# The second attention layer's first 512 destinations: from dense products to row gathers

## The chip, the cores and the metric

The kernel runs on one core of a Trainium2 chip. TensorE multiplies matrices into PSUM, VectorE and ScalarE do elementwise work, GpSimd (POOL in the profile) does small elementwise work and issues indirect DMAs, and SyncE (SP) issues most plain DMAs. The engines run side by side[...] and wait for one another through semaphores. The metric is the device time of one execution in microseconds (us), as a median over runs. Before the change it is 1865.05 us (three runs, 1863.82 to 1865.54).

## The reference

A graph has N = 3125 nodes with 256 features and 103125 edges (50000 random pairs in both directions, and a loop at each node), sorted by destination. A node thus has 33 incoming edges on average. Four blocks follow one another: three attention layers (GAT), a mixture of 16 experts, a plain graph sum, and a top-1 mixture of 8. Only the second attention layer changes. One such layer is

```python
h = x @ W;  el = h @ al;  er = h @ ar
e = leaky_relu(el[src] + er[dst], 0.2)
alpha = softmax of e over the edges of each dst
out = segment_sum(alpha[:, None] * h[src], dst) + b
```

With exp taken out of the leaky relu, an edge's weight is a product of a factor of the source and max(tau of the destination, rho of the source), where rho = exp(0.8 el) and tau = exp(-0.8 er); a factor of the destination alone cancels in the softmax. So the layer needs, for each destination, the sum over its edges of max(tau, rho) times the source's row, and the same sum of weights to divide by.

## The kernel before

**Dense layers.** The nodes are cut into 25 tiles of 128 (the last has 53). While layer 1 runs, the kernel counts how many edges lead from each source to each destination and keeps the counts as bytes in SBUF (`counts`). Each layer then treats the graph as dense. It walks over 13 groups of 256 destinations (`GROUPS`; the last has 53), and within a group over the 25 source tiles (`for s in range(NT)` in `dense_attention`). For each source tile VectorE makes `pm` = max(tau, rho) * counts, 128 sources by 256 destinations (line 1310), and TensorE multiplies it in two halves with the source tile's rows `h`, 256 features and one column of weights, into `acc` (line 1313). The buffers for `pm` are six. tau of the next group comes from two transposes at step 18 (`terms`, lines 1250 and 1253).

**Going onward.** When a group is through, `divide` (lines 1339 to 1348) normalises its sums on VectorE during the next group's step 8, and at steps 10 and 13 `onward` transposes each tile, applies relu on ScalarE and calls `put` (lines 1142 to 1149) of the next layer's `Sources`. `put` multiplies by the next weights, clamps the two scores on VectorE (line 1145), and writes rho, the weight column and the scaled row `h` on ScalarE. `h` is a tile of 25 x 257 floats per partition; rho is a tile of its own. The last tile of a layer goes onward at step 10 of the next layer's first group.

**Lists and counts.** `Locator` gathers pieces of the sorted edge list for windows of five destinations, 125 windows at a time: `find` computes where each begins (`at`) and issues two indirect DMAs of 125 rows of 275 integers (line 1590), `finish` decodes them. `Counter` makes one-hot matrices on VectorE (line 1668) and ScalarE, and multiplies them on TensorE into `counts` (line 1683). This takes place ahead of and during layer 1.

**Queues around it.** During layer 1 SP also writes filler rows into the expert buffers (`spare_rows`, line 1727; three writes in each group, released by two small GpSimd writes, line 1320). The router of layer 3 gets its constants by DMA (lines 579 to 585). In layer 3 GpSimd scatters each node's row of 258 floats to two experts (line 676). The order within each engine's queue is not quite that of the source text: the building layer reorders instructions by its own estimate of when each is ready, and what it decides is fixed before the run.

Of the kernel before, what the change touches and what calls it, by code (L numbers as in the profile page):

```python
# [9 lines left out]
F32 = mybir.dt.float32  # L10
F16 = mybir.dt.float16
BF16 = mybir.dt.bfloat16
I32 = mybir.dt.int32
# [3 lines left out]
OP = mybir.AluOpType  # L17
# [705 lines left out]
def routed_experts(tc, x, room, ident, rows, sums, places, w1, w2, w3, load):  # L723
# [10 lines left out]
    with tc.tile_pool(name="rw", bufs=3) as ep, tc.tile_pool(name="rx", bufs=2) as xp, \  # L734
# [99 lines left out]
        def turn_more(slot, xs, s, own):  # L834
            ps = tp.tile([P, nh, P], F32, name="ps_x")
            for j in range(nh):
                nc.tensor.transpose(ps[:, j], s[:, j * P:(j + 1) * P], ident)
            hid = mp.tile([P, nh, P], F32, name="hid1")
            nc.scalar.copy(hid, ps)
            return slot, xs, hid, own  # L840

# [235 lines left out]
TERMS = 18  # L1077
EARLY = 8
SOME = 6
HELD = 64.0  # L1080


# [32 lines left out]

def block(big, d=D):

    return big.tile([P, NT * (D + 1)], F32, name="big")[:, :NT * d].rearrange("p (t d) -> p t d", d=d)


class Sources:
# [2 lines left out]

    def __init__(self, tc, big, small):
        self.nc = tc.nc
        self.h = block(big, D + 1)
        self.rho = small.tile([P, NT], F32, name="rho")
        self.lr = small.tile([P, 2, NT], F32, name="lr")

        for to in (self.h[:, NT - 1], self.rho[:, NT - 1:], self.lr[:, :, NT - 1]):
            self.nc.gpsimd.memset(to, 0.0)

    def put(self, pp, t, r, xTs, w, at=()):


        nc, n = self.nc, len(xTs)
        pss = []
        for i, xT in enumerate(xTs):
            ps = at[i] if i < len(at) else pp.tile([P, D + 2], F32, name="ps_m")  # L1140
            for k in range(KD):
                nc.tensor.matmul(ps[:r], xT[:, k], w[:, k], start=(k == 0), stop=(k == KD - 1))
            pss.append(ps)
        for i, ps in enumerate(pss):
            nc.vector.tensor_scalar(self.lr[:r, :, t + i], ps[:r, D:], -HELD, HELD, op0=OP.max, op1=OP.min)
        nc.scalar.activation(self.h[:r, t:t + n, D], self.lr[:r, 0, t:t + n], AF.Exp, scale=0.2)
        nc.scalar.activation(self.rho[:r, t:t + n], self.lr[:r, 0, t:t + n], AF.Exp, scale=0.8)
        for i, ps in enumerate(pss):
            nc.scalar.activation(self.h[:r, t + i, :D], ps[:r, :D], AF.Copy, scale=self.h[:r, t + i, D:])


def dense_attention(tc, dram, counts, x_in, big, ident, eps, layers, src, dst, rows, high, make_router, over):

# [6 lines left out]
    nc = tc.nc  # L1162
    with tc.tile_pool(name="dw", bufs=1) as cp, tc.tile_pool(name="dwl", bufs=2) as wl, \
         tc.tile_pool(name="dsm", bufs=2) as small:
        top = cp.tile([P, 3], F32, name="top")
        x = block(big)
        with tc.tile_pool(name="dp", bufs=6) as pmp, tc.tile_pool(name="ds", bufs=2) as sp, \
             tc.tile_pool(name="dpa", bufs=2, space=PSUM) as ap_, \
# [8 lines left out]
            ohp = first.enter_context(tc.tile_pool(name="doh", bufs=2))  # L1177
            kp = first.enter_context(tc.tile_pool(name="dpc", bufs=2, space=PSUM))
            counter = Counter(tc, lp, ohp, locator, counts)
            pairs = [range(-(-c // (BATCH * WIN)), -(-(c + n) // (BATCH * WIN))) for c, n in GROUPS]  # L1180


# [76 lines left out]
            for i in range(3):  # L1259
                last = i == 2  # L1260
                bt_i = bt
                if last:
                    wp = third.enter_context(tc.tile_pool(name="ro", bufs=2))
                    rp = third.enter_context(tc.tile_pool(name="ror", bufs=4))
                    zp = third.enter_context(tc.tile_pool(name="rop", bufs=1, space=PSUM))
                    router = make_router(third.enter_context(tc.tile_pool(name="roc", bufs=1)))
                    y_out = block(big)
                    nc.gpsimd.memset(y_out[:, NT - 1], 0.0)
                    nxt, we_n = None, None
                else:  # L1270
                    nxt = Sources(tc, big, small)
                    we_n, bt, products = attention_weights(tc, wl, cp, layers, i + 1, now.rho[:, NT - 1:])
                    products()
                for a, (c, n) in enumerate(GROUPS):
                    tiles = [(q, (c + q) // P, min(P, n - q)) for q in range(0, n, P)]

                    edges = counts_of(counts, a)
                    ahead = list(pairs[a + 1]) if i == 0 and a + 1 < len(GROUPS) else []
                    ready = []
                    tau = tau_next if a else terms(now, 0)  # L1280
                    acc = ap_.tile([P, 2, CHUNK], F32, name="acc")
                    rest = []
                    if last:
# [5 lines left out]
                    for s in range(NT):  # L1289
# [8 lines left out]
                        if n <= P // 2:  # L1298
                            if s % SOME == 0:
                                m = min(SOME, NT - s)  # L1300
                                few = sp.tile([P, SOME, n], F32, name="few")
                                nc.vector.tensor_tensor(few[:, :m], tau[:, None, :n].to_broadcast([P, m, n]),
                                                        now.rho[:, s:s + m, None].to_broadcast([P, m, n]), op=OP.max)
                                nc.vector.tensor_tensor(few[:, :m], few[:, :m], edges[:, s:s + m, :n], op=OP.mult)
                            at = s % 2 * (P // 2)
                            nc.tensor.matmul(acc[at:at + n, 0, :D + 1], few[:, s % SOME], now.h[:, s], start=(s < 2),
                                             stop=(s >= NT - 2))
                        else:
                            pm = pmp.tile([P, PAIR], F32, name="pm")
                            nc.vector.scalar_tensor_tensor(pm[:, :n], tau[:, :n], now.rho[:, s:s + 1],  # L1310
                                                           edges[:, s, :n], op0=OP.max, op1=OP.mult)
                            for j, (q, t, r) in enumerate(tiles):
                                nc.tensor.matmul(acc[:r, j, :D + 1], pm[:, q:q + r], now.h[:, s], start=(s == 0),  # L1313
                                                 stop=(s == NT - 1))
                        while ready and ready[0][0] <= s:
                            counter.add(kp, ready.pop(0)[1])
                        if s == 2 and fills:

                            for e in empties:
                                nc.gpsimd.tensor_scalar(e, tau[:, 0:1], 0.0, None, op0=OP.mult)  # L1320
# [34 lines left out]
                        norm, gate, send = router.group(wp, rp, zp, y_out, tiles[0][1], len(tiles))  # L1355
                        later += [(9 - sooner, norm), (11 - sooner, gate), (14 - sooner, send)]
                    for j, (q, t, r) in enumerate(tiles if not last else []):
                        def onward(j=j, t=t, r=r, rest=rest, nxt=nxt, w=we_n):
                            ps = pp.tile([P, KD, P], F32, name="ps_m")
                            for k in range(KD):  # L1360
                                nc.tensor.transpose(ps[:, k, :r], rest[j][:r, k * P:(k + 1) * P], ident[:r, :r])  # L1361
                            yT = sp.tile([P, KD, P], F32, name=f"yT{j}")
                            nc.scalar.activation(yT[:, :, :r], ps[:, :, :r], AF.Relu)  # L1363
                            nxt.put(pp, t, r, [yT[:, :, :r]], w)
                        later.append((10 + 3 * j, onward))
                    if i == 0 and a == 1:
                        fills, empties = spare_rows(tc, cp, *rows)
                if i == 0:
                    first.close()
                nc.vector.tensor_reduce(top[:, i:i + 1], now.lr, AX.XY, OP.max, apply_absolute_value=True)  # L1370
                now = nxt
            for _, what in later:
                what()
            router.finish(wp, zp, over)
            ps = pp.tile([3, P], F32, name="ps_m")
            nc.tensor.transpose(ps, top, ident)
            most = cp.tile([3, 1], F32, name="most")
            nc.vector.tensor_reduce(most, ps, AX.X, OP.max)
            ps = pp.tile([1, 3], F32, name="ps_m")
            nc.tensor.transpose(ps, most, ident[:3, :3])  # L1380
            nc.vector.tensor_reduce(high, ps, AX.X, OP.max)
            third.close()
    return y_out
# [135 lines left out]
class Locator:  # L1519
# [8 lines left out]
    def __init__(self, tc, cp, dram, src, dst, ident, room):  # L1528
# [36 lines left out]
        def find(j, pp, behind=None):  # L1565
# [8 lines left out]
            for q in range(NHEAD):  # L1574
                nc.tensor.matmul(ps[:PW], less[:rows, q, :PW], one[:rows], start=(q == 0), stop=(q == NHEAD - 1))
            at = cp.tile([P, 1], I32, name=f"at{j}")
            nc.vector.tensor_scalar(at[:PW], ps[:PW], -1.0, 0.0, op0=OP.add, op1=OP.max)
            if j < PARTS - 1:
                nc.vector.tensor_scalar(at[:PW], at[:PW], float(NR - RE // ER), None, op0=OP.min)
            for u, (of, name) in enumerate(self.lists):  # L1580
                if j == PARTS - 1:

                    to = dram.tile([E + RE], I32, name=name)
                    nc.sync.dma_start(to[:E].rearrange("(p e) -> p e", p=rows), of.rearrange("(p e) -> p e", p=rows))
                    none = cp.tile([1, RE], I32, name=name)
                    nc.gpsimd.memset(none, -WIN)
                    nc.sync.dma_start(to[None, E:], none)
                    of = to
                of = of.rearrange("(t e) -> t e", e=ER)
                nc.gpsimd.indirect_dma_start(  # L1590
                    out=self.edges[j][:PW, u], out_offset=None, in_=of,
# [113 lines left out]
                               acc[:, m - after:m])  # L1705


def spare_rows(tc, cp, rows0, rows1):


# [20 lines left out]
def routed(ctx: ExitStack, tc: tile.TileContext, i: dict, out: bass.AP, over):  # L1731
# [12 lines left out]
    with tc.tile_pool(name="counts", bufs=1) as kp:  # L1744
        counts = kp.tile([P, NT * ((len(GROUPS) - 1) * PAIR + 64)], U8, name="counts")
        x = dense_attention(tc, dram, counts, i["x"], big, ident, eps, layers, i["src"], i["dst"], (rows0, rows),
                            over[:, 3:4], lambda cp: Router(tc, cp, ident, eps, iota, count, rows0, sums,
                                                            i["L0_ffn_gate_w"], i["L0_ffn_gate_b"], more), over[:, 0:1])
        with tc.tile_pool(name="s0", bufs=1) as sp:
            ws, wm = (sp.tile([P, KD, D], F32, name="s_" + n) for n in "WM")  # L1750
            hidden = hidden_weights(nc, early, *(i["L1_ffn_" + n] for n in ("W1", "b1", "Wg", "bg")), x[:, 0, 0:1])
# [99 lines left out]
```

## Time and profile before

| what | us |
|---|---|
| median of three runs | 1865.05 |
| the profiled execution | 1866.04 |
| its span (first to last instruction) | 1864.3 |
| layer 1, first to last product of its groups | about 72 to 455 |
| layer 2 | 456.3 to 755.5 |
| layer 3, last product | about 1047 |
| TensorE busy | 1808.2 (97%) |
| VectorE busy | 971.2 (52%) |
| GpSimd busy | 309.6 (17%) |

All times are of one profiled execution. A group of instructions is given with its line, engine, operation, output and inputs, count, busy time, mean duration in ns, and the idle time of its engine just before it with the engine that ended it. One product in fp32 leaves two records, so 3600 records of line 1313 are 1800 products. Matmuls overlap in the pipeline, so the distance from one to the next (0.433 us for 257 columns) says more than the duration of one (0.38).

### The profile page before, as it was taken

What the parts mean: (1) busy time and instruction counts of PE and PEld (TensorE: products, weight loads), DVE (VectorE), ACT (ScalarE), POOL (GpSimd) and SP (SyncE); (2) the same over time, 40 slices, a digit from 0 to 9 for tenths busy, and PEclk for the clock granted to TensorE, in tenths of its full rate; (3) what the DMA queues carried; (4) which work ended last, traced back from release to release, by engine and by line L of the source; (5) the groups of instructions that cost most, each with busy time, mean ns of one, the idle gap of its engine ahead of it and who ended that gap; (6) DMA issues with size and microseconds to landing.
All of it is one profiled execution on the core that took longest, in us unless ns stands there. A gap on an engine that the chain in (4) does not pass through costs nothing. (4 is left out here: it accounts for less than half of the span.)

```text
span 1864.3 us, 27270 instructions
## 1 busy us (share of the span) xinstructions
PE 1808.2 (97%) x9423; PEld 1427.1 (77%) x9423; DVE 971.2 (52%) x2644; ACT 717.5 (38%) x2052; POOL 309.6 (17%) x461
## 2 busy tenths in 40 slices
PE   6999999999999999999999799999989999999997
PEld 4788888887888888788888566666768886555886
DVE  5888888875555555677777622222252222224221
ACT  3766677671011111122222221211138998444221
POOL 4210100000000000133332322333300000222222
PEclk9999999999999999999999899999999999999999
DMA  3111113757000000111111286767430001733664
GB/s 116 33 36 46 48 62 129 312 213 306 1 1 1 1 1 7 41 46 46 46 46 42 76 261 188 213 180 200 91 80 1 1 1 35 245 128 143 219 211 129
DMA packets 105783, 185.42 MB, mean 99 GB/s; under 512 B 10968, under 2 KB 73849, under 8 KB 105600
## 3 DMA queue, kind: packets, MB, share of 16 engines
q1 hardware_dynamic: 74060, 127.06, 20.2%
q0 software_dynamic: 16432, 34.02, 6.9%
q10 hardware_dynamic: 15138, 22.44, 3.7%
q8 instruction: 79, 1.29, 0.3%
q14 instruction: 74, 0.61, 0.1%
HBM read 95.80 MB, written 89.77 MB: 100 GB/s over the span
## 5 line engine op out<-in xcount | busy, mean ns | idle before, releaser
L1313 PE MATMUL acc<-big,pm 128*128 128x257 f32 x3600 | 828.1, 382 | 3.1 <-DVE pm L1310 3.1
L1313 PEld LDWEIGHTS acc<-big,pm 128*128 128x128 f32 x3600 | 667.6, 190 | 94.6 <-DVE pm L1310 4.8
L1310 DVE SCALAR_TENSOR_TENSOR pm<-tau,rho,counts 128x256 f32<-128x256 f32 x900 | 427.5, 487 | 211.1 <-PE acc L1313 203.5
L774 PE MATMUL ps_h<-xsT,w 128*128 128x384 f32 x512 | 168.4, 487 | 0.6 <-ACT xsT L750 0.6
L1440 PE MATMUL acc<-msg,cr 128*128 128x512 f32 (+1 forms) x625 | 157.7, 403 | 0.1
L774 PEld LDWEIGHTS ps_h<-xsT,w 128*128 128x128 f32 x512 | 96.8, 190 | 66.9 <-issue 1.9
L1440 PEld LDWEIGHTS acc<-msg,cr 128*128 128x128 f32 (+1 forms) x625 | 114.7, 185 | 29.1 <-ACT cr L1436 1.2
L1436 ACT ACTIVATE cr<-counts 128x256 fp32r<-128x256 uint8 (+1 forms) x325 | 130.5, 402 | 14.4 <-PE acc L1440 6.9
L1693 ACT CAST counts<-acc_c 128x500 uint8<-128x500 f32 (+1 forms) x155 | 96.0, 678 | 93.9 <-PE acc_c L1683 93.8
L1023 PE MATMUL ps_y<-t_wd,hsT 128*128 x480 | 108.8, 380 | 0.4 <-ACT hsT L1051 0.4
L1668 DVE TENSOR_TENSOR ohk<-iota_k,key 128x2016 f16<-128x2016 f16 (+1 forms) x79 | 94.4, 1195 | 22.2 <-PE acc_c L1683 22.2
L777 ACT ACTIVATE silu<-ps_h 128x384 f32<-128x384 f32 x64 | 31.4, 491 | 182.1 <-PE ps_h L774 182.1
L1363 ACT ACTIVATE yT<-ps_m 128x256 f32<-128x256 f32 (+1 forms) x50 | 18.7, 375 | 214.4 <-PE ps_m L1361 214.4
L1023 PEld LDWEIGHTS ps_y<-t_wd,hsT 128*128 128x128 f32 x480 | 88.8, 190 | 11.6 <-ACT hsT L1051 0.6
L778 DVE TENSOR_TENSOR hid<-silu,ps_h 128x384 f32<-128x384 f32 x64 | 35.5, 554 | 114.4 <-PE ps_h L774 108.9
L1662 ACT ACTIVATE ohs<-iota_s,low 128x128 f16<-128x128 f16 x286 | 94.1, 401 | 0.0
L929 PE MATMUL ps_H<-big,t_w 128*128 128x512 f32 (+1 forms) x224 | 93.1, 552 | 0.7 <-ACT H L931 0.5
L794 POOL DMA_INDIRECT sums<-y,who x48 | 74.9, 1560 | 94.0 <-DVE y L792 70.3
L789 PE MATMUL ps_o<-w,hid 128*128 128x256 f32 x384 | 87.2, 379 | 0.0
L1683 PEld LDWEIGHTS <-ohs 128*128 128x128 f16 x1250 | 77.7, 98 | 10.9
L1683 PE MATMUL acc_c<-ohk,ohs 128*128 128x125 f16 x1250 | 84.5, 218 | 0.0
L789 PEld LDWEIGHTS ps_o<-w,hid 128*128 128x128 f32 x384 | 71.0, 190 | 8.8
(324 smaller groups left out, 1938.9 us busy)
## 6 DMA issues: line engine op xcount, KB each, us to landing
rows<-empty SPq DMA_DIRECT2D x16, 2564.0 KB, 18.6
w<-in_L_ffn_w_dram ACTq DMA_DIRECT2D x42, 512.0 KB, 4.9
hs<-rows SPq DMA_DIRECT2D x29, 641.0 KB, 4.3
big<-in_L_ffn_w_dram SPq DMA_DIRECT2D x30, 512.0 KB, 6.1
rows<-empty SPq DMA_DIRECT2D x16, 516.0 KB, 5.0
t_wd<-in_L_ffn_Wd_dram SPq DMA_DIRECT2D x8, 1024.0 KB, 11.9
xs<-rows SPq DMA_DIRECT2D x15, 387.0 KB, 3.4
bias<-in_L_ffn_bd_dram SPq DMA_DIRECT2D x30, 128.0 KB, 4.0
```

Of the source, the lines that this page charges most:

```text
L774: nc.tensor.matmul(ps, w[:, k, j * P:(j + 1) * P], xsT[:, k], start=(k == 0), stop=(k == KD - 1))
L789: nc.tensor.matmul(ps, hid[:, j, q * P:(q + 1) * P], o[:, j], start=(j == 0), stop=(j == nh - 1))
L929: nc.tensor.matmul(ps[:, :n], a[:, k, j * P:(j + 1) * P], xnT[:, k, c:c + n], start=(k == 0), stop=(k == KD - 1))
L1023: nc.tensor.matmul(ps, hsT[:, j], d[:, ds(e, 1), j, :].rearrange("p o f -> p (o f)"), start=(j == 0), stop=(j == nh - 1))
L1310: nc.vector.scalar_tensor_tensor(pm[:, :n], tau[:, :n], now.rho[:, s:s + 1], edges[:, s, :n], op0=OP.max, op1=OP.mult)
L1313: nc.tensor.matmul(acc[:r, j, :D + 1], pm[:, q:q + r], now.h[:, s], start=(s == 0), stop=(s == NT - 1))
L1436: nc.scalar.activation(cr[:, :n], edges[:, s, :n], AF.Copy, accum_out=seen[:, a * NT + s:a * NT + s + 1])
L1440: nc.tensor.matmul(acc[:r, j].rearrange("p h d -> p (h d)"), cr[:, q:q + r], msg[:, s].rearrange("p h d -> p (h d)"), start=(s == 0), stop ...
L1662: nc.scalar.activation(far[:, i], self.iota_s, AF.Abs, scale=-1.0, bias=self.low32[:, batch, i:i + 1])
L1668: nc.vector.tensor_tensor(to[:, i:tiles].rearrange("p t (x u) -> p t x u", u=2), iota.rearrange("p (x u) -> p x u", u=2)[:, None].to_broad ...
L1683: nc.tensor.matmul(acc[:, u], ohs[:, i], ohk[:, i, :KEYS], start=(t == 0), stop=(t == TW - 1))
L1693: nc.scalar.copy(to[:, :, d0 % PAIR:d0 % PAIR + whole * WIN].rearrange("p s (u d) -> p u s d", u=whole), acc[:, :whole])
```

## The change

In layer 2 (`i == 1`) groups 0 and 1, destinations 0 to 511, are no longer part of the dense loop. They are computed by a new class, `Apart`. Each partition holds one destination of a tile, and one "slot" is one edge of each of the 128 destinations: GpSimd fetches 128 source rows from DRAM, one per partition, by an indirect DMA; VectorE multiplies each row by its destination's coefficient and adds it to an accumulator (one instruction of 257 elements). A destination has 40 slots in its own tile (`OWN`); what a destination has beyond 40 edges goes to a shared tile of up to 128 heavy destinations with 20 slots (`HEAVY`), which is taken first, and is added back through a product with a 0/1 matrix (`expand`). That makes 20 + 4 x 40 = 180 slots, 45 batches of four, and a ring of five batches (`RING`) in SBUF. Unused slots have the coefficient zero, and their rows are fetched all the same.

What the parts do:

- `Sources`: the row of `h` grows from 257 to 258 floats, and rho becomes its last column.
- `save`, after each `put` of layer 1: one SP DMA of the finished 128 x 258 tile to a table in DRAM, 25 in all.
- `bounds`, `rank` and `collect`, ahead of and in layer 1: find where each destination's edges begin and how many there are (six VectorE passes over 125 x 275, a round trip through DRAM), number the heavy ones, and fetch the source numbers (`who`) by five indirect DMAs.
- `begin`, in step 4 of layer 2's first dense group (now group 2): the 0/1 matrices, tau by partition, and which slots are real.
- `fetch`: four indirect DMAs of 128 rows of 258 floats. The first five batches are placed at step 14; each later one when the batch five before it has been used.
- `events`: the slots, placed from step 22 on at every 1.2 steps; `finished` divides, and sends each of the four tiles onward.
- Small ones: `hid1` reuses the tile it was transposed from, one `none` tile in place of two, a fourth column in `top` that flags a graph whose degrees don't fit the slots.

The diff, cut:

```diff
+ROW = D + 2
+APART = 2
+FEW = 2 * APART
+OWN = 40
+HEAVY = 20
+SLOTS_OF = [(FEW, HEAVY)] + [(t, OWN) for t in range(FEW)]
+BATCH_OF = 4
+RING = 5
+START = 22
+PACE = 1.2
+FETCH = 14
+BEGIN = 4
...
-        self.h = block(big, D + 1)
-        self.rho = small.tile([P, NT], F32, name="rho")
+        self.h = block(big, ROW)
+        self.rho = self.h[:, :, D + 1]
...
+            apart = Apart(tc, cp, dram, locator, *count, ident, top)
+            steps = apart.rank(pp, counter.iota_s)
+            prepare = {(2, 20): apart.bounds}
+            prepare.update({at: lambda: next(steps, None) for at in RANK})
...
+                apart_now, now_apart = i == 1, []
+                if apart_now:
...
+                    now_apart += apart.events(finished)
                 for a, (c, n) in enumerate(GROUPS):
+                    if apart_now and a < APART:
+                        continue
...
-                    tau = tau_next if a else terms(now, 0)
+                    tau = tau_next if a > (APART if apart_now else 0) else terms(now, a)
...
+                        if i == 0 and (a, s) in prepare:
+                            prepare[a, s]()
+                        if apart_now and (a, s) == (APART, BEGIN):
+                            apart.begin(hp, hq, pp, now.lr)
+                        if apart_now and (a, s) == (APART, FETCH):
+                            for b in range(RING):
+                                apart.fetch(b)
+                        while now_apart and now_apart[0][0] <= (a - APART) * NT + s:
+                            now_apart.pop(0)[1]()
...
+    def save(self, sources, t, r):
+        self.nc.sync.dma_start(self.table[t * P:t * P + r], sources.h[:r, t])
...
+    def fetch(self, b):
+        nc = self.nc
+        row = self.hp.tile([P, BATCH_OF, ROW], F32, name="apart_row", bufs=RING)
+        for j in range(BATCH_OF):
+            q = b * BATCH_OF + j
+            nc.gpsimd.indirect_dma_start(
+                out=row[:, j], out_offset=None, in_=self.table[:, :],
+                in_offset=bass.IndirectOffsetOnAxis(ap=self.who[:, q:q + 1], axis=0), bounds_check=N - 1,
+                oob_is_err=False)
+        self.ring[b] = row
+
+    def events(self, finished):
...
+        def batch(b, t):
+            row = state["row"] = self.ring.pop(b)
+            co = state["co"] = self.hp.tile([P, BATCH_OF], F32, name="apart_co", bufs=2)
+            nc.vector.scalar_tensor_tensor(co, row[:, :, D + 1], self.tau[:, t:t + 1],
+                                           self.real[:, b * BATCH_OF:(b + 1) * BATCH_OF], op0=OP.max, op1=OP.mult)
+
+        def slot(j, first):
+            row, co = state["row"], state["co"]
+            if first:
+                state["acc"] = self.hp.tile([P, D + 1], F32, name="apart_acc", bufs=2)
+                nc.vector.tensor_scalar(state["acc"], row[:, j, :D + 1], co[:, j:j + 1], None, op0=OP.mult)
+            else:
+                nc.vector.scalar_tensor_tensor(state["acc"], row[:, j, :D + 1], co[:, j:j + 1], state["acc"],
+                                               op0=OP.mult, op1=OP.add)
...
+        for t, n in SLOTS_OF:
+            for k in range(n):
+                b, j = divmod(q, BATCH_OF)
+                if j == 0:
+                    made.append((g, lambda b=b, t=t: batch(b, t)))
+                made.append((g, lambda j=j, first=(k == 0): slot(j, first)))
+                if j == BATCH_OF - 1 and b + RING < batches:
+                    made.append((g, lambda b=b: self.fetch(b + RING)))
+                if t < FEW and k == 20:
+                    made.append((g, lambda t=t: expand(t)))
+                q, g = q + 1, g + PACE
```

## The prediction

> **What bounds the kernel now.** I read the page's busy line first: TensorE is nearly full over the whole span, and GpSimd nearly empty.
>
> ```profile
> PE 1808.2 (97%) x9423; PEld 1427.1 (77%) x9423; DVE 971.2 (52%) x2644; ACT 717.5 (38%) x2052; POOL 309.6 (17%) x461
> ```
>
> An average over stages says little about one layer, so next the table of windows over 50 us stretches, in the second layer. Columns: stretch, length, busy us (records) of PE, weight loads, VectorE, ScalarE, GpSimd, granted clock, DMA share, GB/s.
>
> ```profile
> 480.00:530.00 50.00, 50.00 (x238) 43.59 (x237) 28.31 (x68) 5.15 (x18) 0.00 (x0) 1.00 0.00 1
> 680.00:730.00 50.00, 50.00 (x239) 43.57 (x238) 27.78 (x65) 5.15 (x18) 0.00 (x0) 1.00 0.00 1
> ```
>
> TensorE is busy all 50 us at full clock, VectorE 28 of 50, GpSimd and the DMA engines nothing. The groups of instructions agree: VectorE's pm waits for TensorE's matmuls, TensorE hardly ever for pm.
>
> ```profile
> L1313 PE MATMUL acc<-big,pm 128*128 128x257 f32 x3600 | 828.1, 382 | 3.1 <-DVE pm L1310 3.1
> L1310 DVE SCALAR_TENSOR_TENSOR pm<-tau,rho,counts 128x256 f32<-128x256 f32 x900 | 427.5, 487 | 211.1 <-PE acc L1313 203.5
> ```
>
> The timeline gives the layer's ends: its first product and that of layer 3. In between lie 299.2 us.
>
> ```profile
> 456.29 8.95 PE L1313 MATMUL acc<-big,pm 128*128 128x257 f32 x40 [1.06 <-DVE pm L1310]
> ...
> 755.47 8.95 PE L1313 MATMUL acc<-big,pm 128*128 128x257 f32 x40 [1.06 <-DVE pm L1310]
> ```
>
> In the steady part of that timeline pm starts every 0.867 us; that is one source tile, two 128x257 products. 300 such steps are 260.1; 25 tiles going onward cost 1.09 each (0.22 transposes, 0.87 two products), 27.3; the small last group's 25 products at 0.238 (20 records, two per product, in 2.38 us) 6.0; 13 tau pairs at 0.22, 2.9. Sum 296.3; the other 2.9 are waits at the start.
>
> **The new operation's price.** No gather of this shape is in the trace. GpSimd's groups show two relatives; after the bar: busy us, mean ns.
>
> ```profile
> L676 POOL DMA_INDIRECT rows<-row,g_to x50 | 50.5, 1009 | 41.1 <-DVE pm L1310 23.7 <-issue 10.7 <-DVE g_to L669 3.0
> L794 POOL DMA_INDIRECT sums<-y,who x48 | 74.9, 1560 | 94.0 <-DVE y L792 70.3 <-issue 20.7 <-DVE hid L778 2.3
> L1590 POOL DMA_INDIRECT counts<-in_src_dram,at x4 | 6.1, 1517 | 1.2 <-issue 1.2
> ```
>
> L676 scatters 128 rows of exactly the new row's 258 floats; L1590 gathers, but 125 rows of 275. GpSimd's timeline shows two in a row 0.30 us apart, whatever they are:
>
> ```profile
> 802.26 0.98 POOL L676 DMA_INDIRECT rows<-row,g_to  x1 [0.30 <-issue]
> 803.55 0.98 POOL L676 DMA_INDIRECT rows<-row,g_to  x1 [0.30 <-issue]
> ...
> 123.69 1.28 POOL L1590 DMA_INDIRECT counts<-in_dst_dram,at  x1 [42.28 <-DVE at L1579]
> 125.28 1.28 POOL L1590 DMA_INDIRECT counts<-in_src_dram,at  x1 [0.30 <-issue]
> ```
>
> So the cadence, C, is 1.29 to 1.31 by the scatter, 1.58 and more by the gathers (1.28 to 1.5, one 2.06, plus 0.30).
>
> [...] L676 takes 1.0 us on GpSimd, its median from issue to landing is 2.6; C is thus GpSimd's time alone. [...] L676 runs beside pm and spreads only from 0.97 to 1.09, so I add 0.02. [...] the trace's L1450 (both inputs SBUF, 256 elements) has a median of 424. I take 0.425 per slot.
>
> **The change, part by part.**
>
> *Removed from TensorE:* 2 groups x 25 steps x 0.867 = 43.4, and two tau pairs, 0.4. *Added:* 4 expand products at 0.43, 1.7, and begin's transposes and tiny products, below 1. If all else hides, layer 2 is 299.2 - 43.8 + 2.7 = 258: the most to be had is 41 us.
>
> *VectorE in layer 2:* 250 pm at 0.407 (eight in a row took 3.26) = 102; 180 slots at 0.425 = 77; 45 coefficient instructions at 0.17 = 8; divides, clamps and the small group about 21. Sum 208 in 258 us, 81%. In the first layer VectorE is busy 44 of 50 us with TensorE still full, so its load doesn't bind.
>
> *GpSimd:* 180 gathers, each one instruction, in a queue that was empty. At C = 1.31 they are 236 us. What matters is when they may run, so I took the built program's order of VectorE instructions. The 180 slots don't stand evenly; they are four runs: 60 between the 24th and the 71st pm, none for 36 pm, 40 up to the 137th, none for 19, 40 up to the 186th, none for 17, 40 up to the 232nd of 250. Within a run a slot stands every 0.75 to 0.8 steps, and a slot whose row hasn't landed holds every pm behind it, hence TensorE, which has six pm in stock (about 5 us).
>
> The chain, from the layer's first product:
> - The first gather waits for the last saved tile. In the trace that tile's ScalarE copy ends at 468.06; with the save's landing (2.4 us for a 128 KB load on SP) that is +14.3. SP's row fills ahead of it are paced by GpSimd's two tau-gated writes per group, and 25 saves of 129 KB add little.
> - 80 gathers back to back: to 14.3 + 104.8 = 119.1. Slot 60's row is in hand by 96, the run ends at about 102.
> - Then 36 pm without a slot at about 0.93 (with onward tiles) take until 136. The ring holds 20 rows, so GpSimd stops at gather 80 until slot 64 frees a batch, at 139: 20 us idle.
> - 100 gathers more, 131 us, with 3 us of smaller stops: 273. In the later gaps the ring has room, and GpSimd stays the pace.
> - Landing 3, and the last four slots, which wait for their batch's last row, with four pm between, 4 to 5: 280.
> - Then 18 steps (15.6), the small group (6.0), five onward tiles (5.4), tau: 28. Sum 308, with the 2.4 of start waits 310.5.
>
> Layer 2 thus becomes 11.5 longer instead of 41 shorter. Above C = 1.25 each 0.1 costs 16 to 18 us; the layer breaks even at about C = 1.23.
>
> *Before layer 1:* bounds adds six passes over 125x275 at 0.5 with their readouts and one at 0.35, and rank some ten small ones at 0.15. The order puts the passes where VectorE has almost no gap (20 to 34 us, ahead of the second half's normalisation). Between 0 and 5; I take 3. In layer 1 the five who gathers hide in GpSimd's 92% idle time.
>
> *Moved:* the router's constants and spare rows, loaded at 427, now wait in SP for the release of the slots' memory, at about +280. They have 28 us plus the first group of layer 3; a gate load took 13 to land. At nothing; uncovered it would be about 5.
>
> *rho inside h, rows of 258, hid1 in place, one none tile:* same instruction counts, at nothing.
>
> Sum: the profiled execution took 1866.0 (span 1864.3 and 1.7 around it); 1866.0 + 11.5 + 3 = 1880.5. The median of the runs is 1.0 below that execution, so **1880**.
>
> **Rivals.**
> - *GpSimd keeps pace, TensorE stays the bound* (other side). For it: GpSimd is empty, a row is only 1 KB, and a gather may be cheaper than a scatter. Against: the 0.30 gap alone leaves 0.9 for the instruction. It decides at C = 1.21 in the total. At C = 1.0 the same chain gives a layer of 273, total 1842; fully hidden, 1866 - 41 + 3 - 1 = 1827.
> - *A gather costs what the trace's gathers cost*, C = 1.58 to 1.6: 270 more ns on 180 gathers, less idle in the first gap; layer about 355, total 1922 to 1926. For it: direction is what these share with the new one. Against: odd row count, other width.
> - *VectorE becomes the bound:* a slot would have to take 0.70 before VectorE fills 258 us, and 0.93 before it eats the whole gain. With gathers hidden and slots at 0.75 the layer is 266, total 1836. The 424 ns row speaks against it.
> - *The skip doesn't take effect:* the loop continues past groups 0 and 1 before any product is issued, and the built order has 250 pm in layer 2, so no.
>
> **Chances.** Scatter-like gather (C 1.25 to 1.45) 0.48, own range 1868 to 1902; trace-gather price 0.24; faster through C below 1.21 0.15; near break-even 0.06; slower otherwise (contention with VectorE, C above 1.7) 0.07. A measurement of this kernel can tell about 0.2% (3.7 us) from no change. Faster 0.15, same 0.06, slower 0.79. The range runs from the break-even side to the gather price: 1860 to 1930.
>
> **What would show it.** Layer 2's TensorE idle before products, near zero now, should be some 50 us, ended by VectorE, and VectorE's in turn by landings of the gathered rows. GpSimd's gather group should read x180, about 1.0 us, gaps of 0.30, one hole of some 20 us after the 80th. Slots near 0.43. If GpSimd shows many holes, the ring and not C sets the pace; if its mean is below 0.9, or TensorE still has no waits, I am wrong on the sign.

## The result, and the profile after

The changed kernel takes **1937.6 us** (median of four runs, 1935.5 to 1946.5) against 1864.4 before: a ratio of **1.040, 95% interval [1.037, 1.044]**. I had forecast 1880 with a range of 1860 to 1930: the sign was right, the size far too small. The profiled execution below is the longest of the four, 1946.5, span 1944.7; the sums are made against it.

The table of windows of the changed kernel, for the stretches shown of before (columns as there):

```profile
480.00:530.00 50.00, 33.77 (x118) 25.75 (x118) 25.53 (x72) 2.46 (x9) 39.26 (x36) 0.82 0.39 95
680.00:730.00 50.00, 41.48 (x190) 33.99 (x189) 34.84 (x96) 3.67 (x13) 32.71 (x31) 1.00 0.29 78
```

TensorE has fallen from 50 busy us of 50 to 34 and 41, and GpSimd, empty before, works 33 to 39. The groups of instructions:

```profile
L1354 PE MATMUL acc<-big,pm 128*128 128x257 f32 x3400 | 814.2, 391 | 52.8 <-DVE pm L1351 26.9 <-issue 19.6 <-DVE apart_acc L1908 3.8
L1351 DVE SCALAR_TENSOR_TENSOR pm<-tau,big,counts 128x256 f32<-128x256 f32 x850 | 400.5, 487 | 184.1 <-PE acc L1354 128.4 <-remote 42.3 <-PE ps_m L1155 5.2
L1884 POOL DMA_INDIRECT apart_row<-apart_rows,apart_who x180 | 198.1, 1100 | 132.8 <-DVE apart_acc L1908 68.4 <-issue 50.0 <-DMA apart_rows<-big 11.7
L1908 DVE SCALAR_TENSOR_TENSOR apart_acc<-apart_row,apart_co,apart_acc 128x257 f32<-128x257 f32 x175 | 84.6, 483 | 0.6
L1899 DVE SCALAR_TENSOR_TENSOR apart_co<-apart_row,apart_tau,apart_real 128x4 f32<-128x4 f32 x45 | 10.0, 224 | 59.3 <-DMA apart_row<-apart_rows,apart_who 56.1 <-issue 3.2
```

As forecast, VectorE waits for landings (L1899, 56 us) and TensorE for pm. Not as forecast: GpSimd itself waits 68 us for the slots to free its ring (L1908), where I had 23, and VectorE's pm waits 42 us for "remote", a releaser that the profile can't name. The ends of layer 2, by TensorE's timeline:

```profile
458.99 7.19 PE L1354 MATMUL acc<-big,pm 128*128 128x257 f32 x32
...
833.52 1.79 PE L1354 MATMUL acc<-big,pm 128*128 128x257 f32 x7 [1.06 <-DVE pm L1351]
```

Layer 2 lasts 374.5 us, 75.3 more than before; ahead of it 2.7 are added, and from layer 3 on 2.4 (span less start of layer 3: 1111.2 against 1108.8). Together 80.4 of the 80.5 between the two profiled executions. So the question is layer 2, where I had 310.5. GpSimd's timeline shows where it stood still for more than 2 us:

```profile
475.96 1.16 POOL L1884 DMA_INDIRECT apart_row<-apart_rows,apart_who  x1 [11.65 <-DMA apart_rows<-big]
564.97 1.02 POOL L1884 DMA_INDIRECT apart_row<-apart_rows,apart_who  x1 [6.36 <-DVE apart_acc L1908]
615.20 1.14 POOL L1884 DMA_INDIRECT apart_row<-apart_rows,apart_who  x1 [22.22 <-DVE apart_acc L1908]
688.14 1.01 POOL L1884 DMA_INDIRECT apart_row<-apart_rows,apart_who  x1 [18.32 <-DVE apart_acc L1908]
763.40 1.13 POOL L1884 DMA_INDIRECT apart_row<-apart_rows,apart_who  x1 [20.90 <-DVE apart_acc L1908]
```

I had forecast the hole at 615; those at 688 and 763 I had ruled out. Each of them follows a gap without slots that lasted 34 and 31 us, twice what 19 and 17 steps take. What happened in the first of these gaps is in TensorE's timeline:

```profile
644.68 6.75 PE L1354 MATMUL acc<-big,pm 128*128 128x257 f32 x29
651.27 0.38 PE L1411 MATMUL ps_m<-ident,y 128*128 128x128 f32 x2
651.49 1.03 PE L1354 MATMUL acc<-big,pm 128*128 128x257 f32 x4
668.76 2.09 PE L1155 MATMUL ps_m<-we,yT 128*128 128x258 f32 x4 [16.24 <-issue]
```

and, of ScalarE and VectorE, in theirs:

```profile
668.33 0.39 ACT L1413 ACTIVATE yT<-ps_m 128x256 f32<-128x256 f32 x1 [38.34 <-remote]
...
662.68 0.48 DVE L1351 SCALAR_TENSOR_TENSOR pm<-tau,big,counts 128x256 f32<-128x256 f32 x1 [4.37 <-remote]
665.52 0.48 DVE L1351 SCALAR_TENSOR_TENSOR pm<-tau,big,counts 128x256 f32<-128x256 f32 x1 [2.36 <-remote]
671.16 0.48 DVE L1351 SCALAR_TENSOR_TENSOR pm<-tau,big,counts 128x256 f32<-128x256 f32 x1 [5.15 <-PE ps_m L1155]
```

The transposes appear at 651.3, but ScalarE's relu of them only starts at 668.3, with ScalarE free all that time; and VectorE's pm, which need a buffer given back by TensorE, start at 657.1, 662.7, 665.5 and 671.2, where there is no slot to wait for. So TensorE completed its work at several us a step, though nothing in the program that the trace shows held it. GpSimd was issuing gathers back to back up to 669.8, where the ring was full.

### The profile page after: what moved, and what is told of

It is laid out like the page before. It is cut to its first block, busy times and chain, and to the rows that moved or that the text cites. A ratio compares the mean times of both kernels' runs of the same rounds, so it can differ in the third digit from the quotient of the medians.

```text
span 1944.7 us, 27562 instructions
## 1 busy us (share of the span) xinstructions
PE 1802.4 (93%) x9249; PEld 1406.4 (72%) x9249; DVE 1020.1 (52%) x2873; ACT 718.2 (37%) x2053; POOL 511.9 (26%) x644
## 5 line engine op out<-in xcount | busy, mean ns | idle before, releaser
L1354 PE MATMUL acc<-big,pm 128*128 128x257 f32 x3400 | 814.2, 391 | 52.8 <-DVE pm L1351 26.9
L1354 PEld LDWEIGHTS acc<-big,pm 128*128 128x128 f32 x3400 | 642.0, 194 | 155.7 <-DVE pm L1351 34.6
L1351 DVE SCALAR_TENSOR_TENSOR pm<-tau,big,counts 128x256 f32<-128x256 f32 x850 | 400.5, 487 | 184.1 <-PE acc L1354 128.4
L1884 POOL DMA_INDIRECT apart_row<-apart_rows,apart_who x180 | 198.1, 1100 | 132.8 <-DVE apart_acc L1908 68.4
L1155 PE MATMUL ps_m<-we,yT 128*128 128x258 f32 (+1 forms) x232 | 67.6, 411 | 34.9 <-ACT yT L1413 17.6
```

Of the source, the lines that this page charges most:

```text
L1884: nc.gpsimd.indirect_dma_start(out=row[:, j], out_offset=None, in_=self.table[:, :], in_offset=bass.IndirectOffsetOnAxis(ap=self.who[:, q: ...
```

## The experiments

Two suspicions: the rows' pace and the ring (A), or VectorE's own load (B). Where sums become wrong, other nodes go to the later experts and the total moves for that reason: SP's loads of expert weights go from 30 to 96 in the first two runs below, whose totals, forecast at 1826 to 1838, are 2073.5 and 2272.1. There only layer 2 is read, from its first product to that of layer 3.

**Few gathers.** All slots, with 20 of the 180 gathers (cut):

```diff
     def fetch(self, b):
+        if b >= RING:
+            self.ring[b] = self.kept[b % RING]
+            return
...
```

> Only the first 20 of the 180 row gathers are issued; every later slot reads those same 20 rows again (160 gathers are left out, so the second layer's first 512 destinations get wrong sums). All 180 slots, 45 coefficient instructions and their order on VectorE stay. Theory A (the rows come too slowly: one per 1.40 us on GpSimd, and GpSimd stands still while the ring of 20 is full between the runs of slots): VectorE no longer waits, layer 2 falls from about 374 to 258 to 265 us, the total to 1826 to 1834 us. Theory B (the slots themselves hold TensorE: 0.487 us each on VectorE in front of the pm, and TensorE at half clock in the gaps): layer 2 stays above 335 us, the total at 1900 or more.

Layer 2: 274.9 us (454.20 to 729.14). The windows of this run, 550 to 600:

```profile
550.00:600.00 50.00, 50.00 (x239) 43.56 (x239) 40.47 (x110) 6.23 (x22) 0.00 (x0) 1.00 0.00 1
```

With all slots in place TensorE is full. B falls. Of the excess over 258, 12.7 us lie between 470 and 510, while the 20 first gathers ran and VectorE waited 6.5, 2.1 and 3.2 us for rows to land.

**Gathers only.** The other half: rows fetched, never read (cut).

```diff
-                nc.vector.tensor_scalar(state["acc"], row[:, j, :D + 1], co[:, j:j + 1], None, op0=OP.mult)
-            else:
-                nc.vector.scalar_tensor_tensor(state["acc"], row[:, j, :D + 1], co[:, j:j + 1], state["acc"],
-                                               op0=OP.mult, op1=OP.add)
+                nc.vector.tensor_copy(state["acc"], self.src[:, t, :D + 1])
...
```

> All 180 gathers are issued, but nothing reads the rows: 175 slots and 45 coefficient instructions are left out, and each of the five sums is a copy of a tile of h. Theory A: GpSimd runs without a hole, first gather at about 17.5 us into the layer, 180 x 1.31 to 1.40 = 236 to 252 us, so it is done within the 258 us of TensorE's own work: total 1826 to 1838 us. Theory B says the same. Theory C (the gathers disturb the other engines[...]): pm above 0.52 us or products with waits although nobody waits for a row, total above 1850 us.

Layer 2: **472.5 us** (455.00 to 927.49), 98 more than with the slots. This run's windows, and its TensorE timeline:

```profile
550.00:600.00 50.00, 8.32 (x16) 4.68 (x16) 1.94 (x4) 0.39 (x1) 38.35 (x38) 0.50 0.37 101
```

```profile
542.50 2.08 PE L1354 MATMUL acc<-big,pm 128*128 128x257 f32 x4 [9.12 <-issue]
553.70 2.08 PE L1354 MATMUL acc<-big,pm 128*128 128x257 f32 x4 [9.12 <-issue]
570.50 2.08 PE L1354 MATMUL acc<-big,pm 128*128 128x257 f32 x4 [14.72 <-issue]
```

A step takes 11.2 us in place of 0.87 while GpSimd gathers undisturbed at 1.31, and nobody waits for a row. The slowing starts some 13 us after the first gather (472.0) and outlasts the last one (708.1): VectorE's pm, held by TensorE, start at 705.1, 715.6, 721.2 and 724.7, and only from about 733 on at 0.87 again. A and B had both said 258; only C, "the gathers disturb the other engines", survives. It was among my rivals only as a remainder of 0.07, "contention with VectorE", and it is not VectorE that is slow: each pm still takes 488 ns. Nor is there a sign of instructions arriving late: in the changed kernel's own slow stretch, from 650 to 672, the only DMA packets are those of the gathers (768 packets, 2.11 MB, 96 GB/s).

**Slots spread evenly.** The heavy tile's sum holds one of the two accumulators to the end of the layer, so each destination tile has to wait until the one before has gone onward; by the program's order that parts the runs of slots. Two edits, not tried one by one: the heavy sum gets a buffer of its own, and each batch is tied to the pm of its step.

```diff
-                state["acc"] = self.hp.tile([P, D + 1], F32, name="apart_acc", bufs=2)
+                state["acc"] = self.spare_acc if t == FEW else self.hp.tile([P, D + 1], F32, name="apart_acc", bufs=2)
...
+            nc.vector.scalar_tensor_tensor(held, self.step[:, 0:1], 0.0, self.tau[:, t:t + 1], op0=OP.mult, op1=OP.add)
-            nc.vector.scalar_tensor_tensor(co, row[:, :, D + 1], self.tau[:, t:t + 1],
+            nc.vector.scalar_tensor_tensor(co, row[:, :, D + 1], held,
```

> Same work as the changed kernel, in another order: the heavy tile's sum lies in a buffer of its own, so that a destination tile need not wait for the accumulator of the one before, and the coefficients of each batch read a value of the pm of their step, so that the 180 slots stand evenly, from the 24th to the 239th pm, in place of four runs. 45 tiny VectorE instructions are added. Theory A: no hole in GpSimd's gathers above 5 us; layer 2 = 17.5 to the first gather + 180 x 1.31 to 1.40 + 3 landing + 11 steps and the tail, 21, so 278 to 294 us; total 1846 to 1863 us. Theory B: the slots are the same, total within 15 us of the changed kernel's 1937.

Total 1902.9 us, ratio to before 1.021 [1.020, 1.023]; layer 2 325.9. Stops of GpSimd fell from 68 us to four of 2.3 to 5.9. The gathers now run almost without a stop, and the layer is 17.0 to the first gather, 267.3 to the last, 41.6 from there to layer 3. The forecast's upper end, 294, missed by that tail (24 assumed) and by the four stops, 15.3 together; the pace, 1.41 a gather, is the slow end of what it named.

**One group apart, evenly.** With the same tie:

```diff
-APART = 2
+APART = 1
-PACE = 1.2
+PACE = 2.2
...
-                state["acc"] = self.hp.tile([P, D + 1], F32, name="apart_acc", bufs=2)
+                state["acc"] = self.hp.tile([P, D + 1], F32, name="apart_acc", bufs=3)
```

> Only the first 256 destinations are treated apart (one dense group less in place of two, 100 gathers and slots in place of 180), in the even order of the run before, from the 24th to the 238th of 275 pm; three accumulators. Theory A: 100 gathers x 1.40 = 140 us are hidden under 17 + 215 us of slots' places; layer 2 = 299.2 - 21.9 for the group + 1.5 = 279 us; the prelude costs 2 us more than before the change: total 1846 to 1850 us, faster than before the change. Theory B: the excess of the changed kernel over its 258 us (116 us) falls to 100/180 of it, 64: layer 343 us, total about 1910 us.

Total 1873.5, ratio 1.004 [1.002, 1.005]. The eleven runs fall into two clusters, four of 1863.9 to 1865.7 and seven of 1871.5 to 1875.9, for a reason that no trace here shows; the profiled execution, 1864.0, is one of the four. Its layer 2 is 299.2 (453.27 to 752.42). A was 20 us too low for that layer, and some 25 for the median. The windows:

```profile
490.00:510.00 20.00, 6.23 (x21) 4.88 (x21) 5.06 (x12) 0.38 (x1) 14.36 (x14) 0.66 0.41 96
```

TensorE lost 14 of 20 us while the ring was first being filled with 20 gathers in a row; from 520 on, with four gathers at a time and pauses between, it is full.

**The same with a ring of two.**

```diff
-RING = 5
+RING = 2
```

> As the run with the first 256 destinations apart and the slots spread evenly (1873.5 us), with a ring of two batches in place of five: GpSimd can issue at most eight gathers in a row at the start and four after each batch, with pauses of 3 us and more between. Nothing is left out. Theory C1: without the 20 gathers in a row at the start, the slow stretch from 485 to 511 us goes, layer 2 falls from 294 to 279 to 284 us, the total to 1852 to 1860 us, faster than before the change. Theory A (only the rows' pace counts): a smaller ring gives less lead, layer 2 stays at 290 us or more, the total at 1870 or more.

```profile
490.00:510.00 20.00, 20.00 (x97) 17.41 (x96) 14.64 (x38) 2.57 (x9) 9.68 (x10) 1.00 0.28 61
```

(The 294 in it was counted from too late a start; read at both ends it is 299.2.) The slow stretch is gone: layer 2 283.5 us, 15.7 less than with five batches, total **1850.7 (six runs, 1846.4 to 1854.0), ratio to before 0.993 [0.991, 0.994]**. This version is faster than both kernels, than the one before by 0.7%.

**What about the gathers slows TensorE?** Five kernels like the one in which nothing reads the rows (472.5 us). These, and the two of the next part, ran once each; the four runs of that one lie within 8 us, far less than the differences read here.

```diff
-                out=row[:, j], out_offset=None, in_=self.table[:, :],
+                out=row[:, j, :ROW // 6], out_offset=None, in_=self.table.rearrange("n (u c) -> (n u) c", u=6),
```

> As in the run where nothing reads the gathered rows (175 slots and 45 coefficient instructions left out, five sums copied from h), but each of the 180 gathers moves a sixth of a row, 43 floats, per partition[...]. With wrong sums the later expert layers get other nodes, so only layer 2's length is to be read; it was 468 us with whole rows. Theory C1 (what slows TensorE is GpSimd issuing gathers one after another without a pause, whatever they carry): layer 2 stays above 400 us. Theory C2 (what slows it is the bytes written into memory next to TensorE's operands): layer 2 falls below 300 us.

(The whole-row run, read at both ends, is 472.5, not 468.)

```profile
550.00:600.00 50.00, 50.00 (x239) 43.58 (x238) 28.21 (x69) 6.23 (x22) 38.69 (x37) 1.00 0.13 17
```

Undisturbed, at the same rate of gathers: C1 falls. Layer 2 is 277.5; the 20 over 257 are one wait at the end, where VectorE's first router constant (more_end) waits until 716 for the ring's memory. Half rows and ordered rows have the same wait, plain loads don't. Half rows:

> As the narrow gathers without readers (175 slots and 45 coefficient instructions left out), but half a row, 129 floats, per gather: about 50 GB/s in place of 101 (whole) and 17 (a sixth). If there is a rate up to which nothing is disturbed and it lies above 50 GB/s: layer 2 258 to 280 us, TensorE busy 50 of 50 us. If the slowing grows in proportion to the bytes: 330 to 380 us.

```profile
550.00:600.00 50.00, 50.00 (x239) 43.58 (x238) 28.41 (x69) 6.24 (x22) 38.74 (x38) 1.00 0.20 50
```

Undisturbed at 50 GB/s, 278.9 us. Then plain loads of the same bytes, by SP and (with `nc.gpsimd`) by GpSimd, in place of the indirect one:

```diff
...
+            t = q % (NT - 1)
+            nc.sync.dma_start(row[:, j], self.table[t * P:(t + 1) * P])
```

> As above with whole rows, but the 180 transfers are plain ones issued by SP: each loads a tile of 128 rows of 258 floats of the same table into the same ring, so the bytes are the same and GpSimd has no part in it (the gathers are left out). Theory C1: TensorE is undisturbed, layer 2 is 258 to 265 us. Theory C2: the bytes come at least as fast, layer 2 above 350 us.

```profile
500.00:550.00 50.00, 50.00 (x239) 43.59 (x238) 28.30 (x68) 5.53 (x19) 0.00 (x0) 1.00 0.93 265
```

> The same 180 plain transfers issued by GpSimd in place of SP (the gathers are left out). If it is transfers issued from GpSimd without a pause that slow TensorE, layer 2 is above 350 us here too; if it needs the indirect form[...] layer 2 is 258 to 275 us.

```profile
500.00:550.00 50.00, 50.00 (x239) 43.58 (x238) 28.70 (x68) 5.13 (x18) 46.03 (x88) 1.00 0.81 239
```

Layer 2 is 257.0 us in both: at 240 to 265 GB/s TensorE isn't touched, so bytes written into SBUF are not it (C2 falls), nor is GpSimd as the issuer. What is left are the addresses:

```diff
+        nc.gpsimd.iota(self.who.rearrange("p (a q) -> p a q", q=20), pattern=[[0, self.width // 20], [P, 20]], base=0,
+                       channel_multiplier=1, allow_small_or_imprecise_dtypes=True)
```

> As the run where nothing reads the gathered rows (175 slots and 45 coefficient instructions left out; layer 2 took 472 us), whole rows by the same 180 indirect gathers, but the row numbers are those of a tile in order, 128 neighbouring rows, in place of the graph's random ones. If scattered reading of DRAM is what slows TensorE: layer 2 258 to 280 us. If it is the indirect form with rows of 1 KB, whatever the addresses: above 400 us.

```profile
550.00:600.00 50.00, 50.00 (x239) 43.56 (x239) 28.24 (x68) 6.24 (x22) 38.52 (x38) 1.00 0.35 99
```

The same 180 indirect gathers of whole rows, at the same 99 GB/s, from neighbouring rows: undisturbed, 279.0. So in these runs it took scattered rows of 1 KB, fetched without a pause, to slow TensorE. Two differences aren't parted. The narrow and half rows are also closer together, since the same row numbers then count sixths and halves from the table's start. And the first 20 gathers, the heavy tile's, are scattered only in part: a partition without a heavy destination starts at edge 0, so all of these read one and the same row (77 of 128 partitions by the reference's graph, 101 with one group apart). Reading one row many times may count in that first burst; in gathers-only the slowing was deepest, 11.2 us a step, in the later ones, whose slots are a tile's own edges.

**Back to the changed kernel.** Does this explain its 374.5? Two ways of taking the disturbance away and leaving gathers, slots and order: narrow rows read six times over, and ordered rows.

> The changed kernel with its 180 gathers, 180 slots, ring and order as they are, but each gather moves 43 of a row's 258 floats, and the slots read these 43 six times over (the sums are wrong, the later expert layers get other nodes; only layer 2 is to be read). In the run with narrow gathers and no reader TensorE was not slowed (50.0 of 50 us busy), so here only the rows' pace is left. If my prediction's chain was right and the missing piece is the slowing of TensorE by whole rows: layer 2 is 305 to 320 us, one hole of about 20 us in the gathers, after the 80th, none above 5 us later. If the missing piece is the rows' pace and the ring (theory A): layer 2 stays at 355 us or more with holes of about 20 us after each run of slots (374.5 us with whole rows).

Layer 2: 332.3 us (455.02 to 787.28), between the two forecasts. GpSimd's stops above 2 us, after the start:

```profile
600.24 1.14 POOL L1884 DMA_INDIRECT apart_row<-apart_rows,apart_who  x1 [17.64 <-DVE apart_acc L1908]
660.49 1.01 POOL L1884 DMA_INDIRECT apart_row<-apart_rows,apart_who  x1 [4.46 <-DVE apart_acc L1908]
```

The holes are as my chain had them; of the 22 us over 310.5, pace is 19.5 and the later first gather 2.7 (below).

> The changed kernel with one edit: the row numbers of the gathers are those of tiles in order, 128 neighbouring rows per gather, in place of the graph's random ones (so the sums are wrong and the later expert layers get other nodes; only layer 2 is to be read). Same 180 gathers of whole rows, same slots, ring and order. Theory D (scattered reading of whole rows at 100 GB/s slows TensorE, which delays the next run of slots, which leaves the ring full): layer 2 falls from 374.5 to 325 to 340 us, as with narrow rows (332.3), with one hole of about 18 to 22 us after the 80th gather and none above 6 us later. If the addresses don't matter once slots are in the way: 360 us or more with holes of about 20 us at each of the three gaps.

Layer 2: 334.4 us (456.58 to 790.96), total 1906.5 in its one run.

```profile
603.47 1.12 POOL L1886 DMA_INDIRECT apart_row<-apart_rows,apart_who  x1 [20.05 <-DVE apart_acc L1910]
663.77 1.00 POOL L1886 DMA_INDIRECT apart_row<-apart_rows,apart_who  x1 [4.97 <-DVE apart_acc L1910]
```

One hole of 20, one of 5, none at the third gap. The second and third gap without slots last 22.7 and 18.6 us, against 33.9 and 31.2 in the changed kernel; the first, 36.6 against 36.8, is the same in both, and a stop of 12 us within the first run of slots (545.7 to 557.7) is gone too. Theory D holds.

## Why the prediction was wrong, step by step

Layer 2, us:

| term | forecast | changed kernel | ordered rows |
|---|---|---|---|
| to the first gather | 14.3 | 17.0 | 17.0 |
| gathers, first to last start, without the holes (179) | 234.5 | 251.3 | 253.4 |
| holes and stops | 23 | 66.6 | 24.4 |
| last gather to layer 3 | 38.8 | 39.6 | 39.6 |
| sum | 310.6 | 374.5 | 334.4 |

(Holes are the stops above 2 us less the usual 0.30 each. The forecast's gathers are 179 x 1.31; its tail is 310.5 less the start of the last gather at 271.7.)

- **The price of a gather was right, the pace was not quite.** The median is 1.01 us with gaps of 0.30: the scatter of the same shape was the right row, which was an estimate until this trace, and the rival with the trace's own gathers (1.58) is out. But the mean is 1.10 beside the slots, 1.04 in the undisturbed runs without a reader, and 1.01 in gathers-only, where VectorE too does little. I had added 0.02 for running beside pm, an estimate from the scatter's spread (0.97 to 1.09); the pace came out 0.09 higher still (251.3 / 179 = 1.40), which is 17 us. My own slope (16 to 18 us for 0.1) gives the same.
- **The failed step is "In the later gaps the ring has room, and GpSimd stays the pace".** It rests on steps of 0.93 us in the gaps. They were slowed to 1.8 by the gathers themselves: TensorE late, so pm late, so the next run's slots late, so the ring full. The term "3 us of smaller stops" measured 45, and with ordered rows 5. That is 40 of the 64 us that layer 2 was over. I had priced a gather by its GpSimd time alone and treated the transfer behind it as free: no term of the sum stands for it.
- **Right:** the first hole (22.2 against 20), the tail, the prelude (2.7 against 3), the floor of 258 (257.0 in the plain runs), and that VectorE is not the bound.
- **Small misses:** a slot's record lasts 0.483, not 0.425, but what it takes of VectorE's queue is 0.40, as for a pm (slot at 647.86, pm at 648.26, slot at 648.66), so my 0.425 was if anything high; the first gather waits 2.7 us longer for the last save; the router's constants, taken at nothing, may be part of the 2.4 us from layer 3 on, which were not taken apart.
- **The point forecast would have missed anyway:** without the slowing, the ordered run's layer gives 1866.0 + 35.2 + 2.7 = 1904 (that run's own total is 1906.5), inside the range but 24 above the point. So the sign was not luck: the gathers' chain alone makes the layer longer.

## What to carry to other kernels

Price a gather twice: its time on the issuing engine (here 1.01 us and a gap of 0.30), and what its stream of scattered reads does to engines that share nothing with it in the program (here a layer of 472.5 us in place of 257); a run that issues the transfers and reads nothing shows the second. Where a prefetch ring fills from empty or through a gap, keep the bursts short: a ring of two batches was 15.7 us faster in layer 2 than one of five, and 23 in the medians of the totals. And where slots bunch, look for the buffer that bunches them; here, by the program's order, one accumulator held for the whole layer put the gaps between the runs.

## What the runs showed of the hardware that I had not expected

Scattered gathers of 1 KB rows, back to back at 101 GB/s, slowed TensorE from 0.87 to 11.2 us a step, and a pair of transposes to about half of that: ScalarE reads one at 558.8, inside the interval of 16.8 us shown above, 5.6 more than 11.2. Undisturbed the pair takes a quarter of a step (0.22 against 0.87), but it has half of its instructions. A time per instruction, not per column, would fit that; it is a reading of this one interval. The slowed steps also come back at the same few lengths. In gathers-only, by VectorE's pm:

```profile
659.56 0.48 DVE L1351 SCALAR_TENSOR_TENSOR pm<-tau,big,counts 128x256 f32<-128x256 f32 x1 [10.32 <-remote]
670.76 0.48 DVE L1351 SCALAR_TENSOR_TENSOR pm<-tau,big,counts 128x256 f32<-128x256 f32 x1 [10.71 <-remote]
681.96 0.48 DVE L1351 SCALAR_TENSOR_TENSOR pm<-tau,big,counts 128x256 f32<-128x256 f32 x1 [10.72 <-remote]
693.16 0.48 DVE L1351 SCALAR_TENSOR_TENSOR pm<-tau,big,counts 128x256 f32<-128x256 f32 x1 [10.71 <-remote]
...
715.56 0.48 DVE L1351 SCALAR_TENSOR_TENSOR pm<-tau,big,counts 128x256 f32<-128x256 f32 x1 [10.02 <-remote]
721.16 0.48 DVE L1351 SCALAR_TENSOR_TENSOR pm<-tau,big,counts 128x256 f32<-128x256 f32 x1 [5.12 <-remote]
```

Here it is 11.20 each time, and 5.60 once the gathers are over. The changed kernel above has 5.6, 2.8 and 5.6; with one group apart, between 493.1 and 501.6, it is 2.81, 2.85 and 2.80. Each length is half of the next. A pace set in steps of two would fit that better than chance waits for memory, but this is a guess, and no run tests it.

Half rows at 50 GB/s, ordered rows at 99, plain loads at 265, and whole scattered rows at 62 to 64 GB/s in bursts of four did nothing: TensorE was busy 50.00 of 50 us in the windows of each. The plain loads wrote rows of the same size into the same ring, and with the same gathers the effect follows the addresses in DRAM (472.5 us scattered, 279.0 ordered), so SBUF is not shown to be its place. Where between DRAM and TensorE it arises stays open, and so does whether it is the rate or the unbroken stream that matters: no run kept the rate and broke the stream.

In its slow stretches TensorE was also granted half its clock: 0.50 from 520 to 700 in the gathers-only run, where it was busy 33.7 of 180 us, and 0.50 from 657 to 671 in the changed kernel, busy 2.2 of 14. Over layer 2 the mean was 0.87 in the changed kernel and 0.93 with ordered rows. A low clock also goes with a wait of another kind: in the narrow run TensorE stood idle for 18.6 us before its product at 718.2, for pm, and the window from 700 to 750 has 0.83, after 1.00 in those before. No run tells here whether the low clock is a cause of the slow steps or goes with the idle time. By itself half a clock is a factor of two, and the steps are longer by 13 (11.2 against 0.87).
